# Layer 0 of a four-layer pre-activation block: image laid by row parity, its convolution in 64x64 and 32x32 tiles

## The chip, the cores and the metric

The kernel runs on one core of a Trainium2 chip. The metric is the device time of one execution in microseconds, lower is better. Three runs of the kernel before gave 4473.49, 4481.63 and 4490.72 us; their median is 4481.63 us. In the text below PE is the matrix engine, PEld its weight load, DVE the vector engine, ACT the scalar engine, POOL the general engine, and SP the engine that only issues DMAs. A "q" after an engine's name means its queue: the instructions that wait or issue a transfer and leave the engine itself idle.

## The reference

The input x is 8 images of 128 channels and 96 x 96 pixels in fp32. Four layers follow one another, each as x = x + layer(group_norm(x)) with 32 groups. The change is in layer 0, a deformable convolution (DCNv4) with 8 groups of 16 channels and a 3 x 3 kernel:

```python
x1 = conv_depthwise_3x3(xn, dw_w) + dw_b            # xn = group_norm(x)
x1 = (x1 - mean) * rsqrt(var + eps) * gn_w + gn_b   # mean, var over the whole image
x1 = gelu(x1)
om = einsum('nhwc,oc->nhwo', x1, om_w) + om_b       # 2 offsets and 1 mask for each of 8 x 9 taps
out = sum over taps of mask * bilinear(xn, place of the tap + offsets)
```

Layer 1 is a dense 3 x 3 convolution, layer 2 a depthwise convolution of signs, layer 3 a scan over the 96 rows with a convolution of 9 taps in each step. The change leaves layers 1 to 3 as they are.

## The kernel before

**Stages.** Layer 0 comes first, for all images; layers 1 and 2 follow together, and layer 3 is last. An image of layer 0 goes through two parts. `image` (from line 566) loads it, takes its statistics, normalizes it in place, makes the depthwise convolution `x1` and stores both to DRAM: the normalized image to `xnd`, the convolution to `x1d`. `chunk` (from line 836) then makes the output in 6 chunks per image, 48 in all. A chunk is every sixth row of the image: a partition is one of 16 rows times 8 groups, and the free dimensions are 16 channels and 96 columns.

**A chunk.** It loads its rows of `x1d` (`x1c`, L843), applies the gelu (L847), projects to offsets and masks with matmuls of 128 x 108 weights (L862, shape 128), evicts them (L870) and takes them through DRAM (`omd`, L878 and L885) to bring them to its own partitions. ACT and POOL make interpolation weights of them (`tx`, `ty`, `wx`, L900 to L969). Offsets stay below one pixel, so the bilinear samples of the 9 taps touch a 5 x 5 neighbourhood; for each of these 25 places DVE multiplies a shifted window of `xs` (16 channels x 96 columns per partition, loaded from `xnd` at L827) with its weight (L1023). PE adds the 25 products and the residual into one PSUM buffer, `ps_s`, with 32x32 identity tiles, 16 matmuls for each (L988, `add_all`). ACT evicts the sum (`y`, L1055). There are 3 buffers for products (`pr`), 5 for `xs`, and a single `ps_s`.

**The depthwise convolution before.** The image lies in `xq`: a partition is one of 2 bands of 48 rows times 64 channels, the free dimensions are the rows of the band (with one halo row at each end), the 2 halves of the channels and the columns. A chunk of the convolution is 4 rows of each band; an image has 12 (`NST`). Each of the 9 taps is one step (`tap`, L720): 8 matmuls with diagonal 32x32 weights and 384 columns, on 8 of the 16 tiles of the array. In image 0, 4 of the 12 chunks (`FIRST_ON_DVE`) are done on DVE instead (L710, L712), 18 instructions each. The two halves of a result lie in two banks of `ps_w`, a single buffer that the projections and small matmuls share (image 0 alternates it with `ps_s`). One ACT instruction evicts a chunk to `x1` (L751), which also sums it; another squares it for the variance (L758). One DMA of 384 KB stores it (L766). There are 2 buffers `x1`.

**The order.** All of this is written as tasks of a small list scheduler in the kernel file (`Plan`). A task has an engine, an estimated cost, a priority (a due time such as `CH * n` for chunk n, with offsets such as `X1_AT` or `SLOT_AT`), buffers and, on PE, a tile shape. `Plan.order` runs the tasks through a model of the engines and so fixes the order in which each engine's instructions are written; on the chip each engine then goes through its own list in that order. The model charges `SWITCH` (0.2 us) when PE's tile shape changes and prefers a task of the present shape if its priority is within `KEEP` (4.0) of the best. SP issues nearly all transfers of layer 0 in that fixed order too: the loads of the next image (L492), the stores of `x1` (L766), the copies of the normalized image (L679), the loads of `xs`, `x1c` and `om`, and the stores of `omd` and `y`. While chunks of image i run, `image` of i+1 runs beside them.

Of the kernel before, what the change touches and what calls it, by code (L numbers as in the profile page):

```python
# [11 lines left out]
F32 = mybir.dt.float32  # L12
I32 = mybir.dt.int32
AF = mybir.ActivationFunctionType
ALU = mybir.AluOpType
# [4 lines left out]
P = 128  # L20
# [34 lines left out]
FIRST_ON_DVE = (2, 5, 8, 11)  # L55
CH, SHIFT, PE_KEEP = 47.0, 8.6, 4.0
LOAD_AT, NORM_AT, COPY_AT, COPY_LATE, COPY_FROM = -140, -90, -70, 220, 52
CONV_AT, CONV_STEP, CONV_PACE, CONV_GAP = -60, 20, 0.9, 0.0
X1_AT, OM_STEP, SLOT_AT = -95, 2.7, 25
BEHIND, AHEAD, CONV_BEHIND = 40, 60, 40  # L60
HOLD, BEHIND1 = False, 40
LAST_ON_POOL, EACH_ON_POOL, POOL_W = (4, 7, 10, 13, 16, 19, 22), (16,), 20
# [139 lines left out]
def kernel(  # L202
# [66 lines left out]
    gmq = const.tile([P, P], F32, name="gmq")  # L269
    gm4 = const.tile([P, P], F32, name="gm4")  # L270
# [5 lines left out]
    for j in range(NB):  # L276
        for b in range(NB):
            soon.append(lambda j=j, b=b: nc.scalar.dma_start(gmq[half(j), half(b)], c_gmean[half(0), half(0)]))
# [143 lines left out]
    with ExitStack() as ph:  # L422
# [3 lines left out]
        x1d = dram.tile([N, P, HW], F32, name="x1d")  # L426
# [3 lines left out]
        dwq = wp.tile([P, NB, K2], F32, name="dwq")  # L430
        dwbq = wp.tile([P, NB], F32, name="dwbq")
        gnwq = wp.tile([P, NB], F32, name="gnwq")
        gnbq = wp.tile([P, NB], F32, name="gnbq")
        for j in range(NB):
            soon.append(lambda j=j: nc.scalar.dma_start(dwq[half(j), :, :], dw_w.rearrange("(j c) t -> c j t", c=HC)))
            put_off(dwbq[half(j), :], dw_b.rearrange("(j c) o -> c (j o)", c=HC))
            put_off(gnwq[half(j), :], gn_w.rearrange("(j c) o -> c (j o)", c=HC))
            put_off(gnbq[half(j), :], gn_b.rearrange("(j c) o -> c (j o)", c=HC))
        tmp = wp.tile([P, 6, W], F32, name="tmp")
        gq = tmp[:].rearrange("p k w -> p (k w)")[:, 2 * P : 4 * P].rearrange("p (j c) -> p j c", j=NB)  # L440
        for j in range(NB):
            put_off(gq[half(0), j, :], c_gmean[half(j), :])
        junk = wp.tile([P, NB, FB], F32, name="junk")
        zero = tmp[:].rearrange("p k w -> p (k w)")[:, : RS * XW]
        nc.gpsimd.memset(zero, 0.0)
        dwd = wp.tile([P, NB, K2, 32], F32, name="dwd")
# [23 lines left out]
        for name, n, shape, psum, in_order in (  # L470
            ("s", 1, [P, NQ, 512], True, True), ("wb", 2, [P, 512], True, True), ("w", 1, [P, CB, 512], True, False),
            ("xs", 5, [P, GC, XW], False, True), ("pr", 3, [P, GC, W], False, True), ("y", 1, [P, NQ, FB], False, True),
            ("om", 1, [P, 3, K2, W], False, True), ("ty", 4, [P, K2, W], False, True), ("tx", 4, [P, K2, W], False, True),
            ("wx", 2, [P, 3, 3, NS, W], False, True), ("x1", 2, [P, NB, FB], False, False),
            ("x1c", 1, [P, YB, W], False, True), ("oe", 2, [P, YB, W], False, True), 
# [10 lines left out]
        def load_rows(i, lo, hi, on=nc.sync, js=range(NB)):  # L486

            for b in range(NB):
                a, z = (max(lo, RP), hi) if b == 0 else (lo, min(hi, XR - RP))
                top = b * HB - RP  # L490
                for j in js:
                    on.dma_start(xq[half(b), a:z, j, RS : RS + W], x[i, half(j), top + a : top + z, :])  # L492

        def band_rows(ap, c):

            return ap.rearrange("p (b f) -> p b f", b=NB)[:, :, c * FB : (c + 1) * FB]

        free_rows = {}
        smalls = []
        for i in range(2):  # L500
            smalls.append({
                name: wp.tile([P, n], F32, name=f"{name}{i}")
                for name, n in (
                    ("st", NB * NST * 6), ("mv", 2 * NB), ("mean", NB), ("d", NB), ("sd", NB), ("sc", NB), ("bi", NB),
                    ("st1", 2 * NST), ("mv1", 2), ("d1", 2), ("mean1", 1), ("v1", 1), ("sd1", 1), ("scp", 1), ("bip", 1),
                )
            })
        maps = []

        def make_maps(at):  # L510
# [4 lines left out]
            def masks():  # L515
                v.tensor_reduce(gp8[:], by_g(gmean[:]), AX.X, ALU.add)
                v.tensor_reduce(gc8[half(0)], gq[half(0)].rearrange("p j (g c) -> p j g c", g=NG), AX.X, ALU.add)
# [3 lines left out]
                for j in range(NB):  # L521
                    v.tensor_scalar(
                        Lx[half(0), j], gc8[half(0), j].unsqueeze(1).to_broadcast([HC, YB, NG]), 0.25, None, ALU.mult
                    )
# [41 lines left out]
        def image(i, at, before=()):  # L566
# [5 lines left out]
            step = 1 if i else 2  # L572
            for m in range(0, NST, step):
                rows = (0 if m == 0 else RP + m * RB, RP + (m + step) * RB if m < NST - step else XR)
                deps = [t for k in range(m - 1, m + step + 1) for t in free_rows.get((i - 1, k), [])] + list(before)
                when = at + LOAD_AT + 3 * m
                if i:
                    loads += [[task("SP", 2.7, lambda r=rows: load_rows(i, *r), deps, when, lag=0.6, move=1.7)]]
                    continue
                loads += [[  # L580
                    plan.task(e, 2.1, lambda r=rows, on=on, j=j: load_rows(0, *r, on, [j]), [], -1e7 + m, lag=0.6, move=1.7)
                    for j, (e, on) in enumerate((("SP", nc.sync), ("ACT", nc.scalar)))
# [3 lines left out]
            for m in range(NST):  # L586
                for j in range(NB):
# [5 lines left out]
                        loads[m][j : j + 1] if i == 0 else loads[m], at + LOAD_AT + 8 + 3 * m,  # L593
# [4 lines left out]
            def aggr():  # L598
                for j in range(NB):
                    nc.vector.bn_aggr(mv2[:, j, :], st[:, j].rearrange("p a b -> p (a b)"))  # L600

            def means(ps):
                nc.tensor.matmul(ps[:, 0, 0:NB], gmq[:], mv2[:, :, 0], start=True, stop=True)
                for j in range(NB):
                    nc.tensor.matmul(ps[half(j), 1, 1:2], gmq[:, half(0)], mv2[:, j, 0:1], start=True, stop=True)
# [30 lines left out]
            def spread():  # L636
                for j in range(NB):
                    nc.scalar.activation(rvs[half(0), j, :], maskf[half(0), :], AF.Identity, scale=sd[half(0), j : j + 1])

            def to_places(ps):  # L640
                for j in range(NB):
                    nc.tensor.matmul(
                        ps[:, 0, :NF], Lx[half(0), j].rearrange("p y g -> p (y g)"), rvs[half(0), j, :],
# [9 lines left out]
            t = plan.task("ACT", 0.5, spread, [coefs, *maps, *placed[-1:]], when)  # L653
            b5 = plan.buf("w")
            t = plan.task("PE", 0.5, lambda: to_places(b5.tile), [t], when, uses=[b5], lag=0.2)
            placed.append(plan.task("ACT", 1.2, lambda: diagonal(b5.tile), [t] + residuals.get(i - 2, []), when, uses=[b5]))

            every = slice(0, P)
            todo = [(half(1), 0, RP, j) for j in range(NB)]
            todo += [(every, RP + r, RP + r + RB, j) for r in range(0, HB, RB) for j in range(NB)]  # L660
            todo += [(half(0), XR - RP, XR, j) for j in range(NB)]
            norms = []

            def norm(parts, lo, hi, j):
                rows = xq[parts, lo:hi, j, RS : RS + W]
                nc.scalar.activation(
                    rows, rows, AF.Identity, bias=bi[parts, j : j + 1], scale=sc[parts, j : j + 1],
                )

            for k, a in enumerate(todo):  # L670
                norms.append(task(
                    "ACT", 0.7 if a[2] - a[1] == RB else 0.45, lambda a=a: norm(*a), [coefs], at + NORM_AT + 1.5 * k
                ))

            def copy_rows(d):
                r, up = (d - RS) % BR, int(d < RS)
                for b in range(NB):
                    for j in range(NB):
                        nc.sync.dma_start(  # L679
                            xnd[i, d, b * YB // NB + up : (b + 1) * YB // NB + up, half(j), :].rearrange("y c w -> c y w"),  # L680
                            xq[half(b), RP + r : RP + HB : BR, j, :],
# [8 lines left out]
            st1 = small["st1"][:].rearrange("p (k c) -> p k c", k=2)  # L690
            outs, stats1 = [], []
            for c in range(NST):
                on_dve = i == 0 and c in FIRST_ON_DVE
                ps = plan.buf("pr" if on_dve else "s" if i == 0 and c % 2 else "w")
                need = (norms[: NB * (c + 3)] if c < NST - 1 else norms) + (ready if i == 0 else []) + (constants if on_dve else [])
                prev = []

                def banks(j, ps=ps, on_dve=on_dve):

                    if on_dve:  # L700
                        return ps.tile[:].rearrange("p c w -> p (c w)")[:, : NB * FB].rearrange("p (j f) -> p j f", j=NB)[:, j, :]
                    return ps.tile[:, j, :FB]

                def tap_dve(t, j, c=c, banks=banks):

                    r0, c0 = RP - 1 + c * RB + t // 3, RS - 1 + t % 3
                    to = banks(j).rearrange("p (r w) -> p r w", w=W)
                    rows, w = xq[:, r0 : r0 + RB, j, c0 : c0 + W], dwq[:, j, t : t + 1]
                    if t == 0:
                        nc.vector.tensor_scalar(to, rows, w, dwbq[:, j : j + 1], ALU.mult, ALU.add)  # L710
                    else:
                        nc.vector.scalar_tensor_tensor(to, rows, w, to, ALU.mult, ALU.add)  # L712

                def tap(t, ps=ps, c=c):
                    r0, c0 = RP - 1 + c * RB + t // 3, RS - 1 + t % 3
                    for j in range(NB):
                        for b in range(NB):
                            for h in range(2):
                                of, to = b * HC + 32 * h, j * HC + 32 * h
                                nc.tensor.matmul(  # L720
                                    ps.tile[to : to + 32, b, :FB],
                                    dwd[of : of + 32, j, t, :],
                                    xq[of : of + 32, r0 : r0 + RB, j, c0 : c0 + W],
                                    start=(t == 0),
                                    stop=(t == K2 - 1),
# [1333 lines left out]
```

## Time and profile before

| | us |
|---|---|
| median of three runs | 4481.63 |
| the profiled execution, its own time | 4480.05 |
| its span, first to last instruction | 4478.3 |
| start to the first product of layer 0 (L1023) | 196.85 |
| last eviction of layer 0 (`y`) begins | 2431.94 |
| PE, DVE, ACT, POOL busy in the whole span | 4053.2, 3840.8, 2548.9, 3135.7 |

The profile divides the span into 40 slices of 112 us and gives the busy share of each engine in tenths. It lists groups of instructions by line with their total busy time, the mean length of one, and the idle time of the engine just before them with what ended it. The "waits" sum up who waited for whom. A "timeline" gives single instructions or runs of them: start, length, engine, line, operands, count, and in brackets the idle time just before. A matmul in fp32 shows as two records. Some records of matmuls are missing, so the counts of PE are a few per cent low.

### The profile page before, as it was taken

The page shows a single profiled execution, that of the slowest core. Times are in us where ns is not written, and L with a number is a line of the kernel's source. Part 1 is how long each engine was busy: PE and PEld are TensorE (multiplying, and loading weights), DVE is VectorE, ACT ScalarE, POOL GpSimd, SP SyncE. Part 2 cuts the span into 40 slices and gives each one's busy share as a digit, 9 for nine tenths or more (in the row PEclk, how much of TensorE's full clock was granted, in tenths as well). Part 3 has the DMA queues.
Part 4 walks back from the last instruction along what each step waited for, and adds up shares of the span by engine and source line. Part 5 has one row for each costly group of instructions (what it writes and reads, how often), then busy time and mean ns, then how long its engine had stood idle before and what let it go on. Part 6 is the DMA issues. An engine that isn't in the chain of part 4 may idle for free. (4 is left out here: it accounts for less than half of the span.)

```text
span 4478.3 us, 168905 instructions
## 1 busy us (share of the span) xinstructions
PE 4053.2 (91%) x75910; PEld 2588.5 (58%) x75910; DVE 3840.8 (86%) x4733; ACT 2548.9 (57%) x3683; POOL 3135.7 (70%) x2207
## 2 busy tenths in 40 slices
PE   4598999989989999999866999899999979999999
PEld 2254554555545546455322555455555548999999
DVE  5599999999999999999997488888888867888887
ACT  3545647457575465654542378777887773333332
POOL 0287887887978878788797499899999971222222
PEclk9798999999999999999998999999999989999999
DMA  7765756658567585563622222232323223232231
GB/s 150 194 170 152 203 148 174 180 145 219 144 173 188 138 221 144 157 189 115 184 88 70 59 69 70 70 75 69 80 70 76 59 48 111 92 107 100 99 113 71
DMA packets 756924, 558.03 MB, mean 125 GB/s; under 512 B 616705, under 2 KB 739218, under 8 KB 750050
## 3 DMA queue, kind: packets, MB, share of 16 engines
q1 hardware_dynamic: 723458, 505.33, 41.9%
q10 hardware_dynamic: 32368, 40.25, 2.7%
q8 instruction: 598, 9.80, 0.9%
q0 software_dynamic: 368, 1.57, 0.1%
q14 instruction: 132, 1.08, 0.1%
HBM read 291.39 MB, written 255.66 MB: 122 GB/s over the span
## 5 line engine op out<-in xcount | busy, mean ns | idle before, releaser
L1023 DVE TENSOR_TENSOR pr<-ps_wb,xs 128x1536 f32<-128x1536 f32 x1193 | 2005.3, 1748 | 120.8 <-PE ps_s L988 87.9
L988 PE MATMUL ps_s<-pr,idr 32*32 32x384 f32 x38176 | 1484.4, 504 | 162.3 <-DVE pr L1023 124.6
L988 PEld LDWEIGHTS ps_s<-pr,idr 32*32 32x32 f32 x38176 | 677.1, 104 | 644.5 <-DVE pr L1023 350.3
L720 PE MATMUL ps_w<-xq,dwd 32*32 32x384 f32 x12672 | 889.6, 494 | 27.6 <-issue 19.9
L1543 PE MATMUL pv_C<-dC,km 128*128 128x384 f32 x1920 | 683.1, 493 | 26.9 <-DVE vn L1566 13.6
L1673 DVE SCALAR_TENSOR_TENSOR pd_C<-xqC,w2s,pd_C 128x768 f32<-128x768 f32 x546 | 554.7, 1016 | 68.1 <-ACT pd_C L1701 38.8
L1909 POOL TENSOR_TENSOR xtD<-xtD,cr 128x384 f32<-128x384 f32 x192 | 192.5, 1003 | 587.1 <-ACT cr L1908 525.1
L935 POOL TENSOR_TENSOR ty<-ty,om 128x864 f32<-128x864 f32 x142 | 289.6, 2040 | 426.5 <-ACT ty L908 250.1
L1543 PEld LDWEIGHTS pv_C<-dC,km 128*128 128x128 f32 x1920 | 354.6, 190 | 322.1 <-issue 58.3
L720 PEld LDWEIGHTS ps_w<-xq,dwd 32*32 32x32 f32 x12672 | 399.9, 104 | 212.2 <-issue 111.8
L960 POOL TENSOR_TENSOR wx<-wx,tmp 128x576 f32<-128x576 f32 x284 | 403.4, 1421 | 22.3
L1529 POOL TENSOR_TENSOR dC<-ywC 128x392 f32<-128x392 f32 x384 | 356.2, 951 | 78.7 <-PE pv_C L1543 51.4
L1970 PE MATMUL ps_b<-tr,km 128*128 128x192 f32 x2304 | 407.5, 325 | 0.7 <-DVE tr L1955 0.7
L1970 PE MATMUL ps_a<-tr,km 128*128 128x192 f32 x2304 | 405.9, 324 | 0.0
L958 POOL TENSOR_TENSOR tmp<-tx,ty 128x576 f32<-128x576 f32 x284 | 404.1, 1423 | 0.0
L1690 POOL TENSOR_TENSOR ptC<-ptC,ptC 128x768 f32<-128x768 f32 x222 | 402.1, 1822 | 1.7 <-ACT ptC L1681 1.6
L941 POOL TENSOR_TENSOR wx<-tx,ty 128x864 f32<-128x864 f32 x142 | 290.0, 2042 | 149.1 <-ACT tx L907 131.6
L1970 PEld LDWEIGHTS ps_b<-tr,km 128*128 128x128 f32 x2304 | 381.0, 189 | 0.7 <-ACT sd_oC L1809 0.7
L1970 PEld LDWEIGHTS ps_a<-tr,km 128*128 128x128 f32 x2304 | 380.0, 188 | 0.0
L1011 ACT ACTIVATE ps_wb<-wx 128x480 f32<-128x480 f32 x240 | 136.5, 569 | 409.5 <-DVE pr L1023 365.5
L862 PE MATMUL ps_w<-x1c,omg 128*108 128x384 f32 x768 | 319.9, 542 | 50.1 <-ACT x1c L847 28.6
L1978 ACT ACTIVATE m<-ps_b 128x192 f32<-128x192 f32 x192 | 63.6, 331 | 494.6 <-PE ps_b L1970 494.4
(245 smaller groups left out, 6157.1 us busy)
## 6 DMA issues: line engine op xcount, KB each, us to landing
xs<-xnd SPq DMA_DIRECT2D x80, 800.0 KB
omd<-oe SPq DMA_DIRECT2D x96, 648.0 KB
om<-omd SPq DMA_DIRECT2D x48, 1296.0 KB
xnd<-xq SPq DMA_DIRECT2D x192, 200.0 KB
x1c<-x1d SPq DMA_DIRECT2D x48, 768.0 KB
y<-y SPq DMA_DIRECT2D x192, 192.0 KB
x<-oC SPq DMA_DIRECT2D x192, 192.0 KB
out<-xtD ACTq DMA_DIRECT2D x24, 1536.0 KB
```

Source lines behind the costliest of these rows:

```text
L720: nc.tensor.matmul(ps.tile[to : to + 32, b, :FB], dwd[of : of + 32, j, t, :], xq[of : of + 32, r0 : r0 + RB, j, c0 : c0 + W], start=(t == ...
L862: nc.tensor.matmul(ps.tile[:HM, b, :FB], omg[:, m * HM : (m + 1) * HM], rows[:, f0 : f0 + FB], start=True, stop=True)
L941: lambda on, s: on.tensor_tensor(flat(wx.tile[:, v, :, 1 : NS - 1]), flat(grid(tx)), flat(grid(ty)), ALU.mult),
L958: on.tensor_tensor(part, flat(grid(te)[:, :, ks : ks + 2]), flat(grid(ty)[:, :, ks : ks + 2]), ALU.mult)
L960: on.tensor_tensor(to, to, part, ALU.add)
L988: nc.tensor.matmul(total.tile[32 * f : 32 * f + 32, r, :FB], weights(rows32, f), of(rows32, f), start=first, stop=last)
L1023: nc.vector.tensor_tensor(pr.tile[:], wb.tile[:, sx * W : (sx + 1) * W].unsqueeze(1).to_broadcast([P, GC, W]), slot.tile[:, :, sx : sx + W ...
L1529: lambda k=k, a=a, b=b, op=op: nc.gpsimd.tensor_tensor(d.tile[:, k], yw.tile[:, a : a + CR - 1 : 2, :], yw.tile[:, b : b + CR - 1 : 2, :], op,
L1543: nc.tensor.matmul(flat(ps), w, d.tile[:, k, :, x_ : x_ + W], start=(x_ == 0), stop=(x_ == 2))
L1673: nc.vector.scalar_tensor_tensor(view, rows8(src, t, h), w[:, t : t + 1], view, ALU.mult, ALU.add)
L1690: lambda a=parts[0], b=pt: nc.gpsimd.tensor_tensor(a.tile[:], a.tile[:], b.tile[:], ALU.add),
L1970: nc.tensor.matmul(ps[:, at_f : at_f + nf], km[:, k, t, :], tr[:, par, :, v : v + HW2], start=(t == 0), stop=(t == NT - 1),)
```

## The change

**Layout.** A partition of `xq` is now one of 2 quarters of a channel half times 2 row parities times 32 channels; the free rows are pairs of rows (48 of them, and a halo of one pair at each end). The halo rows of the bands are gone, and so are the normalizations of them (32 small ones over all images).

**Convolution.** A chunk is 4 pairs of rows. A pair has both its rows in a group of 64 partitions, so the taps that stay within the pair are made by 3 steps (`near`, one per column shift) of 4 matmuls with 64x64 weights; the taps that reach the pair above or below are 3 steps (`over`) of 8 matmuls with 32x32 weights. 6 steps stand for 9, or, counting the two records of an fp32 matmul, 12 for 18. All 12 chunks of image 0 are on PE; the DVE path is removed. The planner prices a `near` step at 0.66 and an `over` step at 0.8 (before: 0.8 for a tap).

**Eviction, store, loads.** The two banks of a chunk now hold channel quarters with different biases, so the bias is left out of the eviction and put into the statistics (`aggr1`, `spread1`, `sum1`, `mid1`, `end1`), and the eviction is two ACT instructions of half the size. A chunk is stored by 4 DMAs instead of 1, `x1c` is loaded by 2 instead of 1. The loads of images 1 to 7 are issued in lumps of 8 DMAs for two chunks (before: 4 DMAs for one). The copies to `xnd` stay 4 DMAs for each sixth of the rows. The setup writes 12 small copies (`dwp`) ahead of its 18 diagonal pieces.

**Constants of the plan.** They are in the diff. Some of the new code is inert with the constants given: `STATS_ON_ACT` is False, `PAIR` is 1, `EACH_ON_POOL` is empty, `GATE` is 12 while `m` ends at 10, and `range(SLOTS_FROM, BR + 2 * RS)` is `range(10, 10)`.

```diff
-FIRST_ON_DVE = (2, 5, 8, 11)
-CH, SHIFT, PE_KEEP = 47.0, 8.6, 4.0
-LOAD_AT, NORM_AT, COPY_AT, COPY_LATE, COPY_FROM = -140, -90, -70, 220, 52
-CONV_AT, CONV_STEP, CONV_PACE, CONV_GAP = -60, 20, 0.9, 0.0
-X1_AT, OM_STEP, SLOT_AT = -95, 2.7, 25
+CONV_COST = 0.66, 0.8
+CH, SHIFT, PE_KEEP = 47.0, 8.2, 4.0
+LOAD_AT, NORM_AT, COPY_AT, COPY_LATE, COPY_FROM = -140, -90, -20, 220, 52
+CONV_AT, CONV_STEP, CONV_PACE = -60, 18, 0.9
+X1_AT, OM_STEP, SLOT_AT = -110, 2.7, 35
...
-            ("x1c", 1, [P, YB, W], False, True), ("oe", 2, [P, YB, W], False, True), 
+            ("x1c", 1, [P, YB, W], False, True), ("oe", 2, [P, YB, W], False, False), 
...
+        def load_rows(i, lo, hi, on=nc.sync, hs=range(2)):
+
+            for h in hs:
+                for p in range(2):
+                    for j in range(NB):
+                        on.dma_start(
+                            xq[quarter(2 * h + p), RP + lo : RP + hi, j, RS : RS + W],
+                            x[i, j * HC + h * QC : j * HC + (h + 1) * QC, 2 * lo + p : 2 * hi : 2, :],
+                        )
...
-                need = (norms[: NB * (c + 3)] if c < NST - 1 else norms) + (ready if i == 0 else []) + (constants if on_dve else [])
+                need = (norms[: NB * (c + 2)] if c < NST - 1 else norms) + (ready if i == 0 else [])
...
-                def tap(t, ps=ps, c=c):
-                    r0, c0 = RP - 1 + c * RB + t // 3, RS - 1 + t % 3
+                def near(t, ps=ps, c=c):
+
+                    r0, c0 = RP + c * RB, RS - 1 + t
                     for j in range(NB):
-                        for b in range(NB):
+                        for h in range(2):
+                            nc.tensor.matmul(
+                                ps.tile[half(j), h, :FB],
+                                dwn[half(h), j, t].rearrange("p e c -> p (e c)"),
+                                xq[half(h), r0 : r0 + RB, j, c0 : c0 + W],
+                                start=(t == 0),
+                                stop=False,
+                            )
+
+                def over(t, ps=ps, c=c):
+
+                    c0 = RS - 1 + t
+                    for j in range(NB):
+                        for p in range(2):
+                            r0 = RP + c * RB + 1 - 2 * p
                             for h in range(2):
-                                of, to = b * HC + 32 * h, j * HC + 32 * h
+                                of = quarter(2 * h + p)
                                 nc.tensor.matmul(
-                                    ps.tile[to : to + 32, b, :FB],
-                                    dwd[of : of + 32, j, t, :],
-                                    xq[of : of + 32, r0 : r0 + RB, j, c0 : c0 + W],
-                                    start=(t == 0),
-                                    stop=(t == K2 - 1),
+                                    ps.tile[quarter(2 * j + 1 - p), h, :FB],
+                                    dwo[of, j, t],
+                                    xq[of, r0 : r0 + RB, j, c0 : c0 + W],
+                                    start=False,
+                                    stop=(t == 2),
                                 )
...
+                for k in range(6):
+                    prev = [task(
+                        "PE", CONV_COST[k // 3], lambda t=k % 3, tap=(near, over)[k // 3]: tap(t), need + prev,
+                        when + CONV_PACE * k + (CONV_BEHIND - BEHIND if i else 0), uses=[ps], lag=0.5,
+                        shape=HC if k < 3 else QC,
+                    )]
...
+                def evict(c=c, x1=x1, ps=ps):
+                    for h in range(2):
+                        nc.scalar.activation(
+                            x1.tile[:, h, :], ps.tile[:, h, :FB], AF.Identity, accum_out=st1[:, h, c : c + 1]
+                        )
...
+                def store(c=c, x1=x1):
+                    for j in range(NB):
+                        for p in range(2):
+                            nc.sync.dma_start(
+                                x1d[i, j, p].rearrange("(h c) k w -> c h (k w)", h=2)[:, :, c * FB : (c + 1) * FB],
+                                x1.tile[quarter(2 * j + p), :, :],
+                            )
...
+            def load_x1():
+                for j in range(NB):
+                    nc.sync.dma_start(x1.tile[half(j)], x1d[i, j, dy % 2, :, dy // 2 :: BR // 2, :])
...
+            for a in range(2):
+                for e in range(2):
+                    for k, y in enumerate((2, 1, 0) if e else (1, 0, 2)):
+                        to = dwp[quarter(2 * a + e), :, 3 * k : 3 * k + 3]
+                        nc.vector.tensor_copy(to, dwq[quarter(2 * a + e), :, 3 * y : 3 * y + 3])
```

## The prediction

> **What bounds the kernel now.** I first read the busy time of the engines by stage: up to 205 us the pipeline of layer 0 fills, from 205 to 2440 its chunks run, then come layers 1 to 3. Columns: window and its length; PE, PEld, DVE, ACT, POOL busy with counts; PE clock, DMA share, GB/s.
>
> ```profile
> 0.00:205.00 205.00, 95.43 (x1658) 46.76 (x1666) 96.92 (x211) 91.63 (x162) 15.47 (x17) 0.85 0.74 169
> 205.00:2440.00 2235.00, 1995.47 (x52459) 1103.38 (x52444) 2096.48 (x1529) 1249.99 (x1917) 1804.68 (x1229) 0.96 0.59 161
> 2440.00:4478.30 2038.30, 1962.32 (x21808) 1438.35 (x21808) 1647.43 (x2994) 1207.25 (x1605) 1315.55 (x961) 0.98 0.28 81
> ```
>
> The change acts in the first 2440 us only. In the long stage DVE is busy 2096 of 2235 us (94%) and PE 1995 (89%). So DVE bounds it, with PE close behind. Next, the groups of both:
>
> ```profile
> L1023 DVE TENSOR_TENSOR pr<-ps_wb,xs 128x1536 f32<-128x1536 f32 x1193 | 2005.3, 1748 | 120.8 <-PE ps_s L988 87.9
> L988 PE MATMUL ps_s<-pr,idr 32*32 32x384 f32 x38176 | 1484.4, 504 | 162.3 <-DVE pr L1023 124.6
> L720 PE MATMUL ps_w<-xq,dwd 32*32 32x384 f32 x12672 | 889.6, 494 | 27.6 <-issue 19.9
> L862 PE MATMUL ps_w<-x1c,omg 128*108 128x384 f32 x768 | 319.9, 542 | 50.1 <-ACT x1c L847 28.6
> ```
>
> DVE spends 2005 us in the 1193 products, which the change leaves alone, and waits 121 us before them. Only such waits can be won. Third, who ends DVE's waits in the stage:
>
> ```profile
> engine line waited for: us in total, times, longest us
> DVE pr L1023 <- PE ps_s L988: 87.9, 80, 4.6
> DVE pr L1023 <- DMA xs<-xnd: 17.6, 5, 5.9
> DVE pr L1023 <- ACT oe L870: 5.2, 2, 4.3
> DVE pr L1023 <- ACT ps_wb L1011: 4.3, 4, 1.7
> ```
>
> 88 us are waits for PE to free a product buffer. Fourth, DVE's timeline in the last image, beside which no convolution runs:
>
> ```profile
> 2235.84 41.71 DVE L1023 TENSOR_TENSOR pr<-ps_wb,xs 128x1536 f32<-128x1536 f32 x25 [0.96 <-PE ps_s L988]
> 2278.08 41.70 DVE L1023 TENSOR_TENSOR pr<-ps_wb,xs 128x1536 f32<-128x1536 f32 x25 [0.53 <-PE ps_s L988]
> 2320.82 10.08 DVE L1023 TENSOR_TENSOR pr<-ps_wb,xs 128x1536 f32<-128x1536 f32 x6 [1.04 <-PE ps_s L988]
> ```
>
> 25 products take 41.7 us, and a gap of 0.5 to 1.0 us stays at each chunk's end, while ACT empties the single sum buffer. At 0.8 us that is 38 us over 48 chunks. So of the 88 us the convolution causes about 50.
>
> **PE's part.** The price of a tap, and of a change of tile shape, is in PE's timeline (fill of the pipeline; then a chunk):
>
> ```profile
> 57.28 6.03 PE L720 MATMUL ps_s<-xq,dwd 32*32 32x384 f32 x144
> ```
>
> ```profile
> 1012.32 2.76 PE L988 MATMUL ps_s<-pr,idr 32*32 32x384 f32 x96
> 1015.02 1.54 PE L862 MATMUL ps_w<-x1c,omg 128*108 128x384 f32 x4
> 1016.49 1.87 PE L988 MATMUL ps_s<-pr,idr 32*32 32x384 f32 x59
> ```
>
> Nine taps take 6.03 us, 0.67 each, and one 128-wide fp32 matmul two records of 0.32. So a tap costs what one stream of 384 columns costs; its 8 tiles run beside each other. Three sums of products (96 records) take 2.76 us, 0.92 each. For the switch, starts of single records: from the last 32x32 record to the first 128-wide one 0.41 us, from there to the next 32x32 one 1.47, against 0.32 and 4 x 0.32 within one shape. That is 0.09 + 0.19 = 0.28 us for a pair of switches, up to 0.57 where the tail of the first would have lain under the next sum.
>
> *Over* steps have the tiles and records of a tap: 3 x 0.67 = 2.0. *Near* steps, 4 tiles of 64x64, are not in the trace. From below: one stream, 0.64. From above: four streams in a row, 2.56. I take 0.66, since the rows with 8 tiles (0.67) and 16 tiles (0.92) are both far from a sum of their streams. A chunk of convolution then costs 2.0 + 2.0 + 0.3 to 0.6 = 4.3 to 4.6 us. Before it costs 6.0 alone; interleaved with the sums about 5.2, from the best chunks (43.4 us: 26 sums at 0.92, 4 projections with switches about 7.4, remainder 12 for two convolution chunks' worth of 20 taps, 0.6 each). So 0.6 to 1.7 us fall per chunk of convolution; I take 1.1. The 84 chunks beside products make 92 us of PE, 4 points of 2235 us.
>
> The Trainium skill ("TensorEngine Tiling (Array Packing)", Key Properties) speaks against the mix: a change of tiling mode, not merely of tile, drains the engine. The row above shows less than a drain of a whole record (about 0.5 us by the groups). By the rule read so, a pair of switches would cost 1.0 us, a chunk 5.0, and nearly all of PE's gain over 5.2 would be gone; by the row, 1.1 stay.
>
> **What DVE gains.** PE falls from 89% to about 85%. Its delays come where sums queue behind a run of taps, so they shrink, but a near group is a block of 2 us that sums cannot enter, and DVE has 3 product buffers at 1.67 us each. I take 70% of the 50 us: **-35**. At most all 50, at least nothing.
>
> **Transfers and SP.** The store becomes 4 DMAs for 1, `x1c` 2 for 1: per image 36 + 6 more issues. In the trace such an issue takes 0.56 us (median of L766 and L843), so +24 us of SP per image, where SP issues 635 us in 1609 (39%); that becomes 47%. Bytes and row lengths stay: image rows are 384-byte runs in SBUF either way. The cover is SP's slack. Without it, an `xs` load that stands behind a store or behind the lump of 8 loads (8 x 0.79 = 6.3 us, before 3.2) comes late. Against this, `SLOT_AT` asks for `xs` 10 us earlier, `X1_AT` for `x1c` 15 us earlier, and `COPY_AT` puts the copies 50 us later. The copies are what `xs` now waits behind (L679, 155 us of SP in 1609, up to 4.1 us each). Of the 17.6 us I take **-10**; bounds -18 and +60.
>
> **ACT.** The eviction, 0.90 + 0.19 us, becomes two of 0.49 (the row of 128x384 from PSUM in layer 1) + 0.19, so +0.27 x 96 = 26 us; 32 halo normalizations (13.3 us) go. ACT is busy 56% and hides it. Without that cover `ps_w` is held 0.27 us longer per chunk, but its fill is 1.4 us shorter. The changed statistics have as many steps, of 0.2 us each: nothing.
>
> **The fill, to 205 us.** DVE's 72 instructions of convolution (38 us) go and lie on no end: PE does 72 steps before (8 x 9) and 72 after. The next thing late is the store:
>
> ```profile
> ACT x L751 <- DMA x1d<-x: 29.3, 7, 7.6
> ```
>
> PE ends the convolution at 104.9, but the last eviction begins at 119.85, since the two `x1` buffers wait for stores that SP issues between copies and loads, with DMA at 0.7 to 0.9 of its engines. The bytes are the same; stores need 48 issues for 16 (+18 us of SP in about 60). PE finishes earlier by (0.67 x 72 + 12 x 0.3 = 52) against 56 us. Ahead of it, 12 copies of about 0.12 (from the diagonal pieces, 18 in 2.72 us) add 1.5 us and two loads of `dwq` at 0.65 add 1.3. I take **-2**, bounds -15 and +15. The inert code and the reordered `oe` pool cost nothing: no instruction comes of them.
>
> **Sum.** -35 - 10 - 2 = -47. The profiled execution took 4480.05 us (span 4478.3 and 1.75 around it), so 4433; it lies 1.6 below the median, which makes **4435 us**, 1.0% faster.
>
> **Rivals.**
> - *DVE at its floor.* All 50 us, the 17.6 of `xs`, 10 of the small waits and 15 of the fill go: -93, **4389**. For it: PE has 15% slack afterwards. Against: most waits are under 1 us and come from order, not load.
> - *Nothing to win.* Switches cost 0.6 us, near blocks stop the sums for 2 us, and DVE waits as often as now: 4460 to 4500, about **4480**. For it: 94% busy on an engine that the change does not relieve.
> - *SP in order.* Lumps and fourfold stores make `xs` late. It decides once an `xs` load stands more than about 5 us behind its due time, which is 3 products of cover. At 1.5 us in each of 42 chunks: +63, less 0 to 20 from PE: **4530**. For it: 17.6 us of such waits exist already.
> - *64x64 tiles one after another.* A near group costs 7.7, a chunk of convolution 10.2, +5 x 12 = 60 us of PE per image. PE's need per image (156 sums at 0.92, 24 projections at 1.8, 62 of taps: about 250) becomes 310, against a period of 283 now: +27 x 7 = +190, **4670**. Against it: the tiles of 32x32 do run beside each other.
>
> **Chances.** Forecast (4405 to 4458) 0.45, DVE at its floor 0.17, nothing 0.21, SP 0.12, serial tiles 0.05. Faster by over 0.5% (about what a measurement of this kernel can tell from no change) is below 4459: 0.62; within it 0.21; slower 0.17. The range leaves out the serial tiles, the late half of SP's case and the far end of the floor: 4370 to 4515.
>
> **What would show it.** Right: DVE's wait for `ps_s` before products falls from 88 to about 50 us, product time stays 2005, near steps at 0.66 us, the chunk period beside convolution from about 47 to 46. Wrong: near records that start one after another by 0.32 us or more; DVE's wait for `xs` above 40; a first product well away from 196.85; a wait of ACT or `ps_w` in place of PE's.

## The result and the profile after

The kernel after takes 4441.55 us (median of 20 runs, 4430.74 to 4518.5) beside 4479.0 us before: ratio **0.9914, 95% interval 0.9904 to 0.9925**, so 38 us or 0.9% faster; 4435 was forecast. The profiled execution of the kernel after was disturbed in layers 1 to 3 (2109 us from the last `y` to the end, for 2046 before, with the same code), as were those of e3 and e6 below, but not in layer 0, so the kernels are compared up to the last `y`.

By stage, with the columns as before (PE, PEld, DVE, ACT, POOL busy; PE clock; DMA share; GB/s):

```profile
0.00:205.00 205.00, 103.52 (x1503) 43.19 (x1503) 84.64 (x168) 90.19 (x186) 15.44 (x17) 0.85 0.79 173
205.00:2400.00 2195.00, 1890.62 (x46311) 817.11 (x46311) 2074.08 (x1520) 1233.10 (x2061) 1803.22 (x1229) 0.95 0.67 163
```

PE is down from 89% to 86% of the long stage, DVE stays at 94%. The groups:

```profile
L1077 DVE TENSOR_TENSOR pr<-ps_wb,xs 128x1536 f32<-128x1536 f32 x1193 | 2003.0, 1745 | 76.2 <-PE ps_s L1031 63.5
L1031 PE MATMUL ps_s<-pr,idr 32*32 32x384 f32 x38176 | 1322.9, 512 | 216.2 <-DVE pr L1077 177.5
L761 PE MATMUL ps_w<-xq,dwo 32*32 32x384 f32 x4320 | 309.8, 489 | 6.5 <-issue 6.4
L745 PE MATMUL ps_w<-xq,dwn 64*64 64x384 f32 x2160 | 230.4, 522 | 22.1 <-ACT x L783 17.6 <-issue 3.3 <-DMA xnd<-tmp 0.5
```

The products cost what they did (2003 us). The time ahead of them fell from 121 to 76 us. But this group shows only the waits that end at a product; the list of all DVE waits in the stage has two rows that were small before (1.9 and 1.0 us), the readers of small statistics matmuls:

```profile
DVE pr L1077 <- PE ps_s L1031: 63.5, 66, 5.6
DVE mean L656 <- PE ps_w L651: 16.7, 6, 3.3
DVE ymv L1146 <- PE ps_w L1153: 15.5, 5, 5.3
DVE pr L1077 <- ACT ps_wb L1054: 4.9, 3, 3.7
```

The 17.6 us for `xs` are gone; for `mean` and `ymv` 32 us stand where 3 stood.

**Where the time lies** is best told by the starts of the `y` evictions, which cut layer 0 into image 0 (fill and its six chunks), images 1 to 6, and the last image. The last column is what DVE is idle in images 1 to 6; DVE's busy time there is 1584 to 1600 us in every run below, so that column is nearly the whole difference between them.

| kernel | ratio, 95% | image 0 done at | images 1 to 6 | last image | DVE idle, 1 to 6 |
|---|---|---|---|---|---|
| before | 1 | 481.4 | 1705.4 | 245.1 | 113.9 |
| after | 0.9914 (0.9904 to 0.9925) | 474.8 | 1675.4 | 242.1 | 83.6 |
| old constants (e1) | 0.9933 (0.9917 to 0.9949) | 486.0 | 1681.6 | 244.4 | 88.5 |
| before, new constants (e2) | 1.0035 (1.0021 to 1.0048) | 489.0 | 1732.6 | 243.4 | 141.4 |
| nine over steps (e3) | 1.0183 (1.0165 to 1.0202) | 513.0 | 1754.1 | 246.8 | 154.4 |
| the same, old constants (e8) | 1.0230 (1.0206 to 1.0253) | 506.2 | 1765.4 | 249.0 | 169.4 |
| one step (e5) | 0.9915 (0.9899 to 0.9931) | 479.6 | 1683.2 | 243.6 | 92.1 |
| before, six taps (e9) | 0.9862 (0.9841 to 0.9883) | 478.5 | 1646.7 | 245.8 | 62.8 |
| store whole (e4) | 0.9901 (0.9880 to 0.9923) | 487.4 | 1657.1 | 243.0 | 65.6 |
| lag (e6) | 0.9908 (0.9895 to 0.9922) | 474.9 | 1677.1 | 243.7 | 83.4 |
| before, half loads (e7) | 1.0019 (1.0003 to 1.0034) | 477.9 | 1708.6 | 244.4 | 117.0 |
| before, fill reordered (e10) | 1.0056 (1.0035 to 1.0076) | 498.8 | 1721.8 | 241.4 | 129.8 |
| whole and gated (e11) | 0.9922 (0.9900 to 0.9944) | 491.4 | 1669.7 | 241.2 | 74.4 |
| `xs` after `om` (e12) | 0.9933 (0.9908 to 0.9958) | 487.9 | 1663.7 | 242.4 | 69.4 |

So the kernel after gains 6.6 us in image 0, 30.0 in images 1 to 6 and 3.0 in the last: 39.7 together, where the ratio makes it 38.5.

### The profile page after: what moved, and what is told of

It is laid out like the page before. It is cut to its first block, busy times and chain, and to the rows that moved or that the text cites. A ratio compares the mean times of both kernels' runs of the same rounds, so it can differ in the third digit from the quotient of the medians.

```text
span 4501.5 us, 156899 instructions
## 1 busy us (share of the span) xinstructions
PE 3975.4 (88%) x69622; PEld 2294.5 (51%) x69622; DVE 3955.0 (88%) x4681; ACT 2530.5 (56%) x3851; POOL 3153.3 (70%) x2207
## 5 line engine op out<-in xcount | busy, mean ns | idle before, releaser
L1077 DVE TENSOR_TENSOR pr<-ps_wb,xs 128x1536 f32<-128x1536 f32 x1193 | 2003.0, 1745 | 76.2 <-PE ps_s L1031 63.5
L1031 PE MATMUL ps_s<-pr,idr 32*32 32x384 f32 x38176 | 1322.9, 512 | 216.2 <-DVE pr L1077 177.5
L1031 PEld LDWEIGHTS ps_s<-pr,idr 32*32 32x32 f32 x38176 | 517.0, 105 | 827.8 <-DVE pr L1077 504.2
L1970 POOL TENSOR_TENSOR xtD<-xtD,cr 128x384 f32<-128x384 f32 x192 | 212.0, 1104 | 632.2 <-ACT cr L1969 563.3
L2031 PE MATMUL ps_b<-tr,km 128*128 128x192 f32 x2304 | 416.8, 328 | 43.5 <-DVE tr L2016 42.8
L1742 ACT ACTIVATE ptC<-vn,wsg 128x768 f32<-128x768 f32 x318 | 286.1, 928 | 72.4 <-PE pq_C L1719 47.0
L907 ACT ACTIVATE oe<-ps_w,ombc 108x768 f32<-108x768 f32 x192 | 172.6, 899 | 258.2 <-PE ps_w L899 257.6
```

The lines of the kernel that those rows point to most:

```text
L1031: nc.tensor.matmul(total.tile[32 * f : 32 * f + 32, r, :FB], weights(rows32, f), of(rows32, f), start=first, stop=last)
L1077: ) if m > 1 else nc.vector.tensor_tensor(
L2031: nc.tensor.matmul(ps[:, at_f : at_f + nf], km[:, k, t, :], tr[:, par, :, v : v + HW2], start=(t == 0), stop=(t == NT - 1),)
```

## The experiments

The theory at the outset (W in the expectations): PE's lighter convolution is the gain; DVE waits less for it. Its rivals: the new due times are the gain (C), the layout and its loads are (L), or DVE is at a floor of its order (F).

**Constants alone, both ways (e1, e2).**

```diff
-CH, SHIFT, PE_KEEP = 47.0, 8.2, 4.0
+CH, SHIFT, PE_KEEP = 47.0, 8.6, 4.0
-LOAD_AT, NORM_AT, COPY_AT, COPY_LATE, COPY_FROM = -140, -90, -20, 220, 52
+LOAD_AT, NORM_AT, COPY_AT, COPY_LATE, COPY_FROM = -140, -90, -70, 220, 52
-CONV_AT, CONV_STEP, CONV_PACE = -60, 18, 0.9
+CONV_AT, CONV_STEP, CONV_PACE = -60, 20, 0.9
-X1_AT, OM_STEP, SLOT_AT = -110, 2.7, 35
+X1_AT, OM_STEP, SLOT_AT = -95, 2.7, 25
```

That is e1, an edit of the kernel after; e2 is the reverse, made in the kernel before.

> The new layout and convolution with the five constants of the plan as before (SHIFT 8.6, COPY_AT -70, CONV_STEP 20, X1_AT -95, SLOT_AT 25). Theory W (the gain is PE's lighter convolution): 4440 to 4455 us, ratio 0.991 to 0.995 against before; DVE's wait for the sums stays near 63 us. Rival C (the gain is the new due times, which bring x1c, om and xs earlier): 4470 to 4490, ratio 0.998 to 1.003, with waits for xs back at 15 us or more and the first product back near 190 us.

> The kernel before with the five new constants alone. Theory W: 4465 to 4485 us, ratio 0.997 to 1.002; DVE's wait for the sums stays near 88 us. Rival C: 4440 to 4455, ratio 0.991 to 0.995, first product near 170 to 180 us, no wait for xs.

Rival C falls. The new constants make the old kernel slower (1.0035); the new kernel keeps most of its gain without them (0.9933, whose interval touches that of the kernel after). What they do for the new kernel is seen in the waits of DVE in images 1 to 6 of e1:

```profile
DVE pr L1077 <- DMA xs<-xnd: 43.6, 6, 9.0
DVE pr L1077 <- PE ps_s L1031: 35.9, 29, 5.0
```

With the old due times `xs` comes late for 43.6 us (6 times, up to 9 us each). That is the rival of the prediction called *SP in order*: it is real, and the five new constants together keep it away (which of them does was not separated). In e1 it costs its 44 us, but there the waits for PE are lower by some 34 us than in the kernel after (36 for 71, with next to nothing at `mean` and `ymv`), so the balance hardly moves.

**Nine steps for six on the new layout (e3, e8).** The near taps proper in 32x32 tiles would have two row tiles add to one place of a PSUM bank with nothing that orders them; that was not tried, and six more over steps stand in for them (other taps are summed).

```diff
...
-                for k in range(6):
+                for k in range(9):
                     prev = [task(
-                        "PE", CONV_COST[k // 3], lambda t=k % 3, tap=(near, over)[k // 3]: tap(t), need + prev,
+                        "PE", 0.8, lambda k=k, over=over: over(k % 3, first=(k == 0), last=(k == 8)), need + prev,
...
-                        shape=HC if k < 3 else QC,
+                        shape=QC,
...
```

e8 has this and the old constants of e1. In both, and in e5 and e9 below, the sums differ from the reference's, so `set_flag`, the kernel's own test for offsets that reach too far, is set never to start the second path that stands behind layer 0.

> The three near steps are replaced by six more steps of 8 tiles of 32x32 (over steps with the same weights, so the convolution sums other taps than the reference), 9 steps for 6, planned at 0.8 each. The layout, stores and constants stay as in the kernel after. Theory W: PE's time per chunk of convolution goes back to 6 us and the 84 chunks beside products cost some 90 us of PE more; DVE's wait for the sums goes back to 85 to 90 us; 4460 to 4475 us, ratio 0.996 to 0.999. Rival C: 4440 to 4450, ratio 0.991 to 0.9935.

> The nine steps of 32x32 tiles (over steps for the near ones, so other taps are summed than in the reference) on the new layout, now with the old constants of the plan. It completes the table of layout, convolution and constants by images 1 to 6 of layer 0: before 1705 us, before with new constants 1733, after 1675, after with old constants 1682, nine steps with new constants 1754. Theory W (the gain there is the steps, the constants help only the short convolution): 1720 to 1735 for images 1 to 6, as the new layout costs about 20 by itself; time 4490 to 4520, ratio 1.002 to 1.009. Rival L (the layout and its loads gain, and nine steps were bad only with the new constants): 1680 to 1695, time 4455 to 4475, ratio 0.995 to 0.999.

Both are slower than either theory had it, and slower than the kernel before: images 1 to 6 lose 79 us against the kernel after, or 84 against e1. The steps are worth more than the whole gain. DVE's wait for sums there in e8, after 36 in e1:

```profile
DVE pr L1077 <- PE ps_s L1031: 124.4, 99, 6.0
```

PE is busy 1577 us in images 1 to 6 of e8, 1564 in the kernel before; yet DVE idles 55 us more. So with nine steps the new layout with its stores, loads and halved evictions (or the order that the planner finds for them) costs by itself: 60 us in images 1 to 6 with the old constants (e8 beside the kernel before), 21 with the new ones (e3 beside e2). The six steps pay for it. Which part of it costs was not separated.

**Less convolution: one step on the new layout (e5), six taps on the old (e9).** In e5 images 1 to 7 make only the first near step, in e9 only the first six of nine taps; the rest of the convolution is left out.

```diff
...
-                for k in range(6):
+                for k in range(6 if i == 0 else 1):
...
```

```diff
...
-                for t in range(K2):
+                for t in range(K2 if i == 0 else 6):
...
```

> Images 1 to 7 make only the first of the six steps of the convolution (the other taps are left out), image 0 all. That takes some 84 x 3.6 = 300 us off PE's 1890 us in the stage. Theory W, that DVE still waits for a PE which is short of time: DVE's wait for the sums falls from 63 to about 40 us, the 16 us each before the means and the image statistics fall too; 4395 to 4420 us, ratio 0.981 to 0.987. Rival F, that DVE is at the floor of its order and PE's load no longer matters: 4432 to 4445, ratio 0.989 to 0.9925.

> The kernel before, but images 1 to 7 make only 6 of the 9 taps (the last row of taps is left out): 4.0 us of PE per chunk of convolution for 6.0, about as much less as the change has, with the old layout, stores, constants and fill. Theory W (what images 1 to 6 gain is PE's fewer steps): images 1 to 6 take 1670 to 1690 us for 1705, the fill stays at 251.6 to the first y; 4445 to 4465 us, ratio 0.992 to 0.997. Rival L (it comes of the new layout and its transfers): 1700 to 1710, ratio 0.998 to 1.002.

e9 shows W without the new layout: nothing but taps is left out, the fill is as before, and images 1 to 6 fall by 59 us, more than forecast (51 of them are DVE's idle time). What is left of its waits for PE in images 1 to 6:

```profile
DVE pr L1023 <- PE ps_s L988: 45.3, 48, 2.8
```

It was 73 us before, and the 17.6 us for `xs` are gone, though no transfer was added or taken out. That these were PE's too is not shown, for with fewer taps the planner wrote SP's list in another order as well. In the kernel before, the late `xs` stand behind some two dozen copies of the next image. The last twelve, ahead of the wait that ends at 1372.6 us:

```profile
1346.15 13.35 SPq L679 DMA_DIRECT2D xnd<-xq  x12
1359.55 3.23 SPq L1072 DMA_DIRECT2D y<-y  x4
1362.88 0.54 SPq L878 DMA_DIRECT2D omd<-oe  x1
1363.52 4.36 SPq L827 DMA_DIRECT2D xs<-xnd  x2
```

e5 shows the other end. PE and the rest in images 1 to 6 of e5, and then of the kernel after:

```profile
480.00:2163.00 1683.00, 1264.47 (x31232) 458.93 (x31224) 1590.92 (x1180) 986.75 (x1647) 1393.27 (x959) 0.92 0.71 172
```

```profile
475.00:2150.00 1675.00, 1488.90 (x35737) 653.95 (x35718) 1591.42 (x1181) 979.43 (x1652) 1358.39 (x932) 0.95 0.71 172
```

PE does 224 us less, and nothing comes of it (ratio 0.9915), as F has it. But F's reason, that PE no longer matters, is not shown, for PE's clock fell as well (0.92 for 0.95). The clock that the trace records in images 1 to 6 is either 1.00 or 0.50, and 0.50 in spells. One such spell of e5 and the time behind it:

```profile
1155.00:1161.00 6.00, 5.20 (x66) 2.07 (x68) 1.52 (x2) 2.11 (x3) 5.84 (x4) 0.50 0.43 127
1162.00:1168.00 6.00, 6.00 (x136) 2.57 (x134) 5.47 (x5) 2.27 (x3) 5.84 (x6) 1.00 0.40 105
```

PE ahead of the spell, in it and at its end, and the wait of DVE in it:

```profile
1145.99 0.94 PE L1031 MATMUL ps_s<-pr,idr 32*32 32x384 f32 x32 [1.52 <-DVE pr L1077]
1155.80 2.90 PE L899 MATMUL ps_w<-x1c,omg 128*108 128x384 f32 x4 [3.78 <-ACT x1c L884]
1158.62 3.16 PE L1031 MATMUL ps_s<-pr,idr 32*32 32x384 f32 x64
1161.71 1.54 PE L899 MATMUL ps_w<-x1c,omg 128*108 128x384 f32 x4
1160.40 3.42 DVE L1077 TENSOR_TENSOR pr<-ps_wb,xs 128x1536 f32<-128x1536 f32 x2 [4.48 <-PE ps_s L1031]
```

PE idles 3.78 us; then four records of the projection take 2.90 us instead of 1.54, two sums take 3.16 us where one took 0.94, and DVE waits 4.48 us. In images 1 to 6 PE is at half clock for 109 us before, 181 in the kernel after and 256 in e5. DVE's idle time there, split by the clock at that moment:

| | at full clock | at half clock |
|---|---|---|
| before | 93.3 | 20.6 |
| all versions with nine steps (with before, e2, e3, e7, e8, e10) | 93 to 126 | 18 to 44 |
| after | 47.1 | 36.5 |
| all with six steps on the new layout (with after, e1, e4, e6, e11, e12) | 41 to 56 | 22 to 40 |
| six taps on the old (e9) | 46.5 | 16.3 |
| one step (e5) | 32.1 | 60.0 |

DVE idles 6, 3 and 2% of the time at full clock before, after and in e5, but about a fifth of the time at half clock in all three. So at full clock less work on PE does go on to pay, and in e5 the longer time at half clock takes it back. That the half clock causes the waits that fall into it is read from lines like these; no run held the clock up. By place, about half of e5's waits for sums (37 of 72 us in the whole layer) stand before the fourth product of a chunk, when three products wait for the single `ps_s` to be emptied.

**The new waits taken away (e6).** The planner reckons 3 us from a small statistics matmul to its reader:

```diff
+SMALL_LAG = 3.0
...
-                "PE", 0.7, lambda: means(b1.tile), [t, *ready], -1e6, uses=[b1], lag=0.1,
+                "PE", 0.7, lambda: means(b1.tile), [t, *ready], -1e6, uses=[b1], lag=SMALL_LAG if i else 0.1,
```

and likewise for the other four.

> The kernel after, but the planner reckons 3 us between a small statistics matmul and the DVE instruction that reads it (before 0.05 to 0.2), so that DVE's order places one or two products ahead of the reader. Theory O (DVE stands idle 32 us at the image ends before the means and ymv, since PE reaches those matmuls later than the plan believes): these waits go, 4405 to 4420 us, ratio 0.983 to 0.987. Rival B (the wait is only moved to the next wait for a sum, since DVE runs ahead of PE there): 4436 to 4446, ratio 0.9905 to 0.993.

Rival B, exactly. In images 1 to 6 the rows of `mean` and `ymv` are gone, and the wait for sums has grown from 41.7 to

```profile
DVE pr L1078 <- PE ps_s L1032: 68.4, 58, 7.3
```

with 83.4 us of idle DVE for 83.6. The 29 us had only stood at another instruction.

**A chunk stored whole (e4).**

```diff
-        x1d = dram.tile([N, NB, 2, P // 2, HB, W], F32, name="x1d")
+        x1d = dram.tile([N, P, 2, HB * W], F32, name="x1d")
...
+                    nc.sync.dma_start(x1d[i, :, :, c * FB : (c + 1) * FB], x1.tile[:])
...
+                    for h in range(2):
+                        rows = x1d[i, quarter(2 * j + dy % 2), h].rearrange("c (k w) -> c k w", w=W)
+                        nc.sync.dma_start(x1.tile[quarter(2 * j + h)], rows[:, dy // 2 :: BR // 2, :])
```

> The kernel after with the convolution's result laid out in DRAM so that a chunk is stored by 1 DMA (4 in the kernel after) and x1c is loaded by 4 (2): 24 issues of SP fewer per image, 36 in the fill. Theory S (SP's issues cost time, in the fill above all, where two x1 buffers wait for stores): first product 5 to 15 us earlier, 4425 to 4437 us, ratio 0.988 to 0.9905. Rival N (SP has slack and the stores wait for bytes): the same within the order's luck, 4437 to 4448, ratio 0.9905 to 0.993.

The time is the one of theory S (0.9901), but not for its reason: the first product comes 33 us later (202.2), images 1 to 6 are 18 us shorter (15 of them idle time of DVE at half clock: 21.8 us for 36.5), and the sum isn't told apart from the kernel after. The fill shows in SP's timeline, first of e4 and then of the kernel after (start, length, instruction):

```profile
109.47 3.87 SPq L858 DMA_DIRECT2D xs<-xnd  x5
113.43 0.66 SPq L797 DMA_DIRECT2D x1d<-x  x1
114.19 12.95 SPq L502 DMA_DIRECT2D xq<-in_x  x8
127.40 0.52 SPq L797 DMA_DIRECT2D x1d<-x  x1
131.73 1.91 SPq L877 DMA_DIRECT2D x1c<-x1d  x4
```

```profile
112.01 1.43 SPq L880 DMA_DIRECT2D x1c<-x1d  x2
113.48 14.81 SPq L502 DMA_DIRECT2D xq<-in_x  x24
128.59 0.31 SPq L915 DMA_DIRECT2D omd<-oe  x1
129.19 6.35 SPq L502 DMA_DIRECT2D xq<-in_x  x8
135.71 0.30 SPq L915 DMA_DIRECT2D omd<-oe  x1
142.14 0.35 SPq L922 DMA_DIRECT2D om<-omd  x1
```

In e4 five loads of `xs` (800 KB each) and a lump of image loads stand ahead of the last two stores, so `x1c` is issued 20 us later. In the kernel after (and in e1, e5, e6) `xs` comes after `om`.

**The fill by SP's order (e10, e11, e12), and the loads of image 0 (e7).** Two edges were put into the plan of the kernel before (e10, for the loads of image 1 from the fifth on) and of e4 (e11, its last two lumps):

```diff
+                deps += first_om if i == 1 and m >= GATE else []
...
-                outs, at + X1_AT, uses=[x1], lag=0.6, move=3.3,
+                outs + (first_keep if n == 1 else []), at + X1_AT, uses=[x1], lag=0.6, move=3.3,
```

e12 is e4 with the second of these and with `GATE, SLOTS_FROM = 12, 0`, which makes the five `xs` loads wait for the first `om`.

> The kernel before with two edges more in the plan, for SP's order in the fill alone: the loads of image 1 from the third on, by twos of the kernel after, wait for the first om, and the second x1c waits for the first chunk's omd. Theory Q (what the change won in the fill is that SP's list there has the last store, x1c and both omd with nothing that blocks in front of them, not the shape of the tiles): first product 170 to 182 us for 197, layer 0 ends 10 to 20 us earlier; 4460 to 4472, ratio 0.9955 to 0.998. Rival T (the fill is shorter by the 64x64 tiles and the eviction): first product 192 to 200, ratio 0.999 to 1.002.

> The kernel after with the chunk stored whole, as tried alone, and the same two edges for SP's order in the fill (the last two lumps of loads of image 1 wait for the first om, the second x1c for the first chunk's omd). Theory Q: the first product comes at 165 to 178 us (202 with the whole store alone) and the rest stays as with the whole store; 4395 to 4415 us, ratio 0.981 to 0.986. Rival T: the first product stays at 195 to 203, 4425 to 4440, ratio 0.988 to 0.991.

> The kernel after with the chunk stored whole, and in the plan's fill the five xs loads (800 KB each) made to wait for the first om, which keeps them behind the last stores, x1c and both omd in SP's list as they are in the kernel after (with the whole store alone they came ahead of the last stores, and x1c 12 to 20 us later); the second x1c waits for the first chunk's omd. Theory X (the place of those 4 MB in SP's list is what the fill turns on): gelu at 118 to 126 us (139.5 with the whole store alone), first product 165 to 176 (202), the rest as with the whole store, 4400 to 4420 us, ratio 0.982 to 0.987. Rival B (the new order of the lists takes it back later, as it did with the gated loads of image 1): first product early too, but 4430 to 4445, ratio 0.989 to 0.992.

Three misses for the theories; only e12 ends near its rival (4439 us, 0.9933). The first product did come earlier each time (185.7 for 196.8; 182.8 and 182.6 for 202.2), but image 0 was done later than before the edit in e10 and e11 (498.8 for 481.4, 491.4 for 487.4) and at the same time in e12 (487.9). In e12 the gelu came at 125.6 us, as forecast, and image 0 took it back: DVE idles 31.7 us between its first product and the end of image 0, 10.3 in e4. **The first product isn't what the end of image 0 turns on.**

```diff
-                    on.dma_start(xq[half(b), a:z, j, RS : RS + W], x[i, half(j), top + a : top + z, :])
+                    for k in range(2 if i == 0 else 1):
+                        to, of = (quarter(2 * b + k), quarter(2 * j + k)) if i == 0 else (half(b), half(j))
+                        on.dma_start(xq[to, a:z, j, RS : RS + W], x[i, of, top + a : top + z, :])
```

> The kernel before, with each load of image 0 cut into two DMAs of 32 partitions (24 more issues), as the kernel after has them, but of whole neighbouring rows. Theory H (image 0 comes in 7 us earlier because its DMAs are half as tall and more of them are under way): the last row statistics of image 0 end near 35 us for 41, the first product 5 to 8 us earlier than 196.9; 4470 to 4478 us, ratio 0.998 to 1.0. Rival P (it is the parity of the rows, every second row of x, that loads faster): statistics end at 40 to 42 us, ratio 0.999 to 1.001.

The row statistics of image 0 end at 41.4 us (41.0 before, 34.5 after), so it isn't the size of the DMAs that brings image 0 in earlier. (The last of these statistics stand in DVE's list behind set-up instructions, whose small loads follow those of the image.) With the same order of the lists, e7 also tells how well one profile repeats: images 1 to 6 are 3.2 us apart.

## Why the prediction was right, and where it wasn't

**PE's part: right.** PE is busy 75 us less in images 1 to 6 (1564 to 1489), 1.04 us for each of 72 chunks of convolution; 1.1 was taken. The 64x64 tiles run side by side. Steps in the fill, and in flow between sums:

```profile
71.35 2.18 PE L745 MATMUL ps_w<-xq,dwn 64*64 64x384 f32 x24
73.46 2.17 PE L761 MATMUL ps_w<-xq,dwo 32*32 32x384 f32 x48
75.56 2.18 PE L745 MATMUL ps_s<-xq,dwn 64*64 64x384 f32 x24
```

```profile
1049.38 0.94 PE L1031 MATMUL ps_s<-pr,idr 32*32 32x384 f32 x32
1050.26 0.88 PE L745 MATMUL ps_w<-xq,dwn 64*64 64x384 f32 x8
1051.07 0.94 PE L1031 MATMUL ps_s<-pr,idr 32*32 32x384 f32 x32
1051.94 0.88 PE L745 MATMUL ps_w<-xq,dwn 64*64 64x384 f32 x8
```

A chunk takes 4.21 us from one near group's start to the next (71.35 to 75.56), where 4.3 to 4.6 was forecast: 0.2 us over six steps of 0.67, for two changes of mode and the near steps' own surplus. The rule of the Trainium skill that a change of tiling mode drains the engine ("TensorEngine Tiling (Array Packing)", Key Properties), weighed in the prediction at 1.0 us for a pair, would have made that chunk 5.0: the measurement decides against that size. In flow a near step and a sum take 1.68 us together (1050.26 to 1051.94). One sentence was wrong: sums do enter a near group; the planner put the near steps singly between sums.

**DVE's gain: -35 forecast; the total nearly right, the place wrong, and partly by luck.** The wait before products fell by 24 us (87.9 to 63.5, where about 50 was named), and the chunk period from 47.4 to 46.5 us, as named. But `mean` and `ymv` took 29 us more, and e6 shows that this is the same delay of PE. By name, waits for PE in images 1 to 6 hardly moved (73 + 3 before, 42 + 15 + 14 after). What fell is `xs` (17.6) and small waits (some 8). e9 loses `xs` too, but with another order of SP's list, so the terms -35 and -10 can't be told apart here; together they gave -33 (images 1 to 7) for -45. The step that is missing is the clock, a term that the prediction put at nothing: DVE's idle time at full clock fell by 46 us (17.6 of them for `xs`), and at half clock it rose by 16. The total came near because these two partly cancel.

**SP: right in kind.** SP issues 760 us in images 1 to 6 for 649 before, 18.5 more per image (24 forecast). With the old due times this shows as 44 us of waits for `xs` (e1), but as 5 us of idle time in all.

**ACT: right.** Half an eviction takes 0.49 us, and DVE's wait for ACT's `ps_wb` is 4.9 us in the stage (4.3 before).

**The fill: -2 forecast, with "a first product well away from 196.85" named as a sign of error.** It came at 169.5. Image 0 was in 6.5 us sooner, the last eviction ended at 106.7 for 120.8 as stores stood earlier in SP's list, and `om` was issued 21.9 us after the gelu for 31.9, with `xs` out of the way. But of these 27 us 18 were left at the first `y` and 6.6 when image 0 was done. One thing that had not moved is the second chunk's `om`; that it is the cause was not tested. Its first reader on ACT, before and after:

```profile
203.85 0.92 ACT L900 ACTIVATE ty<-om 128x864 f32<-128x864 f32 x1 [1.84 <-DMA om<-omd]
```

```profile
202.40 0.92 ACT L943 ACTIVATE ty<-om 128x864 f32<-128x864 f32 x1 [7.02 <-DMA om<-omd]
```

DVE starts 27 us sooner and idles 28.5 us in image 0 for 7.9. The step that failed is the cost of the fill, read from evictions and PE alone; by luck of the order the error was small.

**Rivals.** *Nothing to win* and *serial tiles* are excluded by the ratio and the near steps. *DVE at its floor* lies 50 us too low; no run has less than 63 us of idle DVE in images 1 to 6, and how much of that is the clock's is said above. *SP in order* is alive in e1. No version here that computes the whole convolution beats the kernel after beyond the intervals; e4 is level with it.

**Open:** which part of the new layout costs the 21 to 60 us that e3 and e8 show, how much of it is left with six steps, how far single orders of the planner scatter (1657 to 1683 us with six steps or fewer on the new layout, 1705 to 1765 with nine on either), and what a PE held at full clock would give.

## What to carry to other kernels

When an engine close behind the bound is relieved, look for its delay at every instruction of the bound engine that reads it, and at the queues that stand behind it, not only in the row that was longest; the sum of idle time over a stretch is what counts. Relief pays until something else sets the waits, and here that was in part the lower clock of the relieved engine itself: when an ablation that leaves most of the work out changes nothing, split the idle time by the granted clock before calling it a floor. An earlier start is worth only what is left at the next thing that is late, so measure the end of the first full round, not its first instruction.

## What the runs showed of the hardware

Image 0 loads faster in the new layout. From 10 to 20 us, before and after:

```profile
10.00:20.00 10.00, 0.00 (x0) 0.00 (x0) 3.98 (x8) 0.00 (x0) 0.00 (x0) 1.00 1.30 180
```

```profile
10.00:20.00 10.00, 0.00 (x0) 0.00 (x0) 6.00 (x13) 0.00 (x0) 0.00 (x0) 1.00 1.05 219
```

180 GB/s became 219 at a lower share of the DMA engines; half-size DMAs of neighbouring rows (e7) stay at 176. Every second row, or the partitions that are filled at one time, may be the reason; it wasn't separated.

The mean granted clock of PE went down as work was taken off it: 0.97 in images 1 to 6 before (92% busy), 0.95 after (89%), 0.92 in e5 (75%). The records behind these means are 1.00 or 0.50 only, with 109, 181 and 256 us at 0.50. The busy share alone doesn't set the mean: e1 has 0.94 and e9 0.96, both at 88%.
